# Attention with a recurrence beside it: where sinks and the fourth far tile are turned within a round

## The chip, the core and the metric

The kernel runs on one core of a Trainium2 chip. The metric is device time in microseconds for one execution. Before the change the median of three runs is 2368.65 us (2368.1 to 2369.14).

## The reference

A block of attention and a gated recurrence, for 4 sequences of 1024 tokens and 1024 channels in fp32. Attention has 16 query heads over 4 key heads of 64 channels, a sliding window of 512 keys, and 4 sink keys that every query sees. Cut to what matters:

```python
xn = _layernorm(x)
# attention
mask = (j <= i) & (j >= i - 511) | (j < 4)      # and causal for the first rows
att = softmax(where(mask, einsum('bkgqd,bkjd->bkgqj', q, k) / 8, -inf))
s = (att @ v) @ Wo.T
# recurrence: on the last token of each sequence, four steps
thought = layer_norm(xn)[:, -1, :] @ agg_w + agg_b
for _ in range(4):
    t = gelu(layer_norm(thought) @ d1_w + d1_b)
    thought = thought + t @ d2_w + d2_b
gate = sigmoid(xn @ gate_w + gate_b)
g = silu(layer_norm(xn + gate * (thought @ bc_w + bc_b)))
out = x + s * g
```

## The kernel before

The program has three stages. The first normalizes x and computes keys, values, queries and gates. The second, which the change touches, computes attention, and beside it the recurrence, whose weights are streamed from memory. The third multiplies by `Wo`, applies the gate and adds x.

**Rounds.** A tile is 128 queries. Attention takes query tiles in pairs (`PAIRED`): a *far* tile, the fifth to eighth of its sequence, whose window has left the start, and a *near* tile, the first to fourth. For a pair it takes 2 pairs of key heads and 2 halves of a group's heads, so 4 rounds for each of 16 pairs, 64 rounds in all. A `Step` is one tile in one round: two query heads for each of two key heads. A far step always has four turned key tiles (the first one holds the leading and the own keys laid over each other by a predicated copy) and four sink keys besides. A near step has 1, 2, 3 or 4 key tiles: the first pair of each sequence has 1, the fourth has 4.

**What a step does.** Line numbers are those of the profile.
- `scores` (L267): products of queries and keys into the PSUM tile `S` (four banks, one buffer). VectorE lays own keys over leading ones (L272), then adds the mask, scales and reduces (L289, with the extreme `nm`); ScalarE takes the exponential and sums it (L294). A far step does it in two halves, `scores((0,))` and `scores((1,))`, both into the one buffer; a near step at once.
- `normalized` (L301, L305): reciprocal of the sums, and the rows `pr` times it, on VectorE.
- `turned(k)` (L312): four 128x128 transposes into one PSUM tile, then a copy to `pT` by ScalarE (L316). For tile 0 of a far step VectorE also makes `lead` from the copy (L322).
- `turned_sinks` (L334): the last 32 columns of four `pr` tiles are multiplied by an identity, each into its own 32 rows of one PSUM tile; ScalarE copies it to `sT` (L339).
- `values(k)` (L344): value products of key tile k into `yp`. `values_apart`: the products with the sinks (L361) and with `lead`.
- `stored` (L374): copy of `yp` by VectorE; each second one is followed by a DMA from GpSimd (L379).

**PSUM.** Turned tiles, turned sinks and the recurrence's own turned or summed results share tag "T" of pool `ps_t`, with two buffers; `S` has four banks, `yp` and the recurrence's sums (`ps_f`) one each. [...]`pT` has four buffers in SBUF, `lead` and `sT` one.

**The recurrence.** `ffn()` is a generator: each unit is either a block of streamed weights (four products of 128x512, each into 32 rows, L685, with the DMA of its block on SyncE's queue, L683), or a turning of summed rows (four transposes, L739) or a mean or variance product (L759). There are 173 units. `filler(slot)` issues what is due; a round has three slots, and units are spread over the first 60 rounds, so nearly every slot has one. The last four rounds have none.

**What sets the order.** Within the attention loop TensorE's order is the order of the program text (`manual_schedule` for that engine). The other engines' orders are set by the scheduler from its own estimates of when inputs are ready. A round interleaves the current far and near step with the scores of the next round's steps, from L897 to L929. The array works in a mode, given in the profile as rows*columns: transposes 128*128, scores 64*128, value products 128*64, sinks' turning and the streamed blocks of the recurrence 128*32.

Of the kernel before, what the change touches and what calls it, by code (L numbers as in the profile page):

```python
# [43 lines left out]
def recurrent_block_kernel(  # L44
# [92 lines left out]
    sink_values, leads = {}, {}  # L137

    def load_kv(b):

        pool = pools["odd" if b % 2 else "first"]
        kT = pool.tile([P, N_KV // 2, TT, P + SINK], F32, tag="kT", name=f"kT{b}")
        v = pool.tile([P, TT, KVD], F32, tag="v", name=f"v{b}")
        for h in range(TT // BLK):
            n, at = b * (TT // BLK) + h, slice(h * BLK, (h + 1) * BLK)
            for m in range(N_KV // 2):
                nc.sync.dma_start(
                    kT[:, m, at, SINK:], k_dram[n][:, m, :].rearrange("p (t k) -> p t k", k=P)
                )
            nc.sync.dma_start(v[:, at, :], v_dram[n])  # L150
        far = WINDOW // P
        nc.gpsimd.tensor_copy(
            kT[:, :, far:, :SINK],
            kT[:, :, 0:1, SINK : 2 * SINK].to_broadcast([P, N_KV // 2, TT - far, SINK]),
        )

        sinks = pools["first"].tile([P, PAIR, KVD], F32, tag="sinks", name=f"sinks{b}", bufs=2)
        nc.gpsimd.memset(sinks, 0.0)
        for g in range(2):
            for r in range(PAIR):  # L160
                end = (2 * g + r + 1) * QUAD
                nc.gpsimd.dma_start(
                    sinks[end - SINK : end, r, :].rearrange("p (m g c) -> p m g c", m=2, g=2)[
                        :, :, g, :
                    ],
                    v_dram[b * (TT // BLK)][:SINK, 0, :].rearrange(
                        "p (m g c) -> p m g c", m=2, g=2
                    )[:, :, g, :],
                )
        kTs[b], vs[b], sink_values[b] = kT, v, sinks  # L170

    def load_q(i):
        qTs[i] = pools["first"].tile([P, N_HEAD // 2, P], F32, tag="qT", name=f"qT{i}", bufs=4)
        n, j = divmod(i, BLK)
        nc.sync.dma_start(qTs[i], q_dram[n][:, :, j * P : (j + 1) * P])
# [44 lines left out]
    class Step:  # L220
# [132 lines left out]
            last = not self.far and k + 1 == len(self.keys)  # L353
            self.added(self.pT.pop(k), vs[self.b][:, self.keys[k], :], k == 0, last)

        def values_apart(self):

            for r in range(PAIR):
                for g in range(2):
                    cols = slice((2 * self.m + g) * HS, (2 * self.m + g + 1) * HS)  # L360
                    nc.tensor.matmul(  # L361
                        self.y[g * HS : (g + 1) * HS, r * P : (r + 1) * P],
                        sink_values[self.b][:, r, cols], self.sT,
                        start=False, stop=False, skip_group_check=True,
                    )
            self.added(self.lead, leads[self.i], False, True)

        def stored(self):
# [23 lines left out]
    def steps_of(tiles, m, rp):  # L392
        return [Step(i, m, rp) for i in tiles]
# [5 lines left out]
    with ExitStack() as a:  # L399
# [193 lines left out]
        for n in range(NBLK):  # L593
# [11 lines left out]
            for kind, w7, part in (  # L605
                (queries, wq7, 0), (queries, wq7, 1), (gates, wg7, 0), (gates, wg7, 1)
            ):
                if n == NBLK - 1 and kind is gates and part == 0:
# [8 lines left out]
                    far, near = steps_of(*order[0])  # L617
# [26 lines left out]
    with ExitStack() as a:  # L644
# [188 lines left out]
        def load_y(n, row):  # L833

            t = ws.tile([P, 2, KH, BT // 2], F32, tag="stream", name=f"y2_{n}_{row}")
            ys.setdefault(n, {})[row] = t
            for j in range(BLK // 2):
                nc.sync.dma_start(
                    t[:, :, :, j * P : (j + 1) * P],
                    y_dram[n * BLK + row * (BLK // 2) + j].rearrange(  # L840
                        "p (h c q) -> p h c q", h=2, c=KH
                    ),
                )
# [3 lines left out]
        def filler(slot):  # L847
            nonlocal ffn_done
            due = FFN_UNITS * (p * SLOTS + slot + 1) // (ffn_steps * SLOTS)
            while ffn_done < min(due, FFN_UNITS + 1):  # L850
                next(ffn_gen, None)
                ffn_done += 1

        with tc.manual_schedule(engines={mybir.EngineType.PE}):
            for p in range(len(order)):
                pair, within = divmod(p, per_pair)
                if within == 0:
                    b, t = divmod(pair, TT // 2)  # L860
                    i = PAIRED[pair][0]
                    own = i % TT
                    leads[i] = px.tile([P, KVD], F32, tag="leads", name=f"leads{i}", bufs=2)
                    nc.vector.tensor_tensor(
                        leads[i], vs[b][:, own - WINDOW // P, :], vs[b][:, own, :], ALU.subtract
                    )
                    if pair + 1 < len(PAIRED):
                        for i in PAIRED[pair + 1]:
                            load_q(i)
                    if t == 1 and b + 1 < B:  # L870
                        load_kv(b + 1)


                if 0 <= p - 2 * DT < 2 * DT:
                    c, g = divmod(p - 2 * DT, 2)
                    m, r = divmod(c, GROUP)
                    h = (2 * m + g) * GROUP + r
                    tc.keep_in_program_order(
                        nc.sync.dma_start(
                            wo_sb[g * HS : (g + 1) * HS, c, :],  # L880
                            wo[h // 4, h % 2 * HS : (h % 2 + 1) * HS,
                               h // 2 % 2 * D : (h // 2 % 2 + 1) * D],
                        )
                    )
                if p > 4 * DT:
                    for dst, minuend, subtrahend in islice(wo_parts, 1):
                        tc.keep_in_program_order(
                            nc.vector.tensor_tensor(dst, minuend, subtrahend, ALU.subtract)
                        )
                if p == ffn_steps:  # L890
                    for _ in ffn_gen:
                        pass
                    for row in range(2):
                        load_y(0, row)
                more = p + 1 < len(order)
                n_near = len(near.keys)
                far.turned(0)  # L897
                far.turned_sinks()
                if more:
                    far_next, near_next = steps_of(*order[p + 1])  # L900
                    far_next.scores((0,))
                for k in (1, 2):
                    far.turned(k)
                filler(0)
                for k in range(3):
                    far.values(k)
                far.turned(3)
                if more:
                    far_next.normalized((0,))
                    far_next.scores((1,))  # L910
                for k in range(min(2, n_near)):
                    near.turned(k)
                filler(1)
                far.values(3)
                far.values_apart()
                far.stored()
                for k in range(2, n_near):
                    near.turned(k)
                if more:
                    far_next.normalized((1,))  # L920
                    near_next.scores(both)
                for k in range(n_near):
                    near.values(k)
                if more:
                    near_next.normalized(both)
                near.stored()
                filler(2)
                if more:
                    far, near = far_next, near_next  # L929
# [276 lines left out]
```

## Time and profile before

| what | value |
|---|---|
| profiled execution, its own time | 2368.6 us |
| its span, first to last instruction | 2366.9 us |
| granted TensorE clock | 1.000 |
| attention stage (first to last transposition of `pr`) | 1039.7 to 1972.2 us |
| transposes t, TensorE | 1664, 245.0 us busy |
| copies pT, ScalarE | 416, 585 ns each |
| masks and reductions, VectorE (L289) | 512, 590 ns each |
| exponentials, ScalarE | 512, 639 ns each |
| normalizing, VectorE (L305) | 512, 437 ns each |
| `lead`, VectorE | 64, 686 ns each |
| y copy, VectorE | 128, 420 ns each |
| sinks' turning, TensorE | 512 records, 64 copies of 261 ns |

The span is what the trace covers; the profiled execution's own time is 1.7 us longer. Matmuls of TensorE are pipelined: their lengths overlap, and what a group takes is read from its first start to the next group's first start. An fp32 product that isn't a transposition shows as two records. The number in brackets behind a row is idle time of the engine just before it, with what ended it.

### The profile page before, as it was taken

To read this page: it belongs to the slowest core of one execution; us is meant where nothing else is said; L and a number is where in the kernel's file an instruction comes from. 1 tells how busy PE (TensorE), PEld (TensorE's weight loads), DVE (VectorE), ACT (ScalarE), POOL (GpSimd) and SP (SyncE) were. 2 spreads that over 40 slices of the span, in tenths; PEclk is the share of its full clock that TensorE was granted. 3 is DMA by queue.
4 is the path that set the end of the run, shared out by engine and by line. 5 is a ranking of instruction groups with operands and counts; after the bars stand their busy time and mean duration, and the time that the engine had idled before them with its cause. 6 is when DMAs were issued, how large, how long until landed. Compare 5 with 4: busy or idle time off the path is not lost.

```text
span 2366.9 us, 31507 instructions
## 1 busy us (share of the span) xinstructions
PE 2324.0 (98%) x11966; PEld 1353.1 (57%) x11966; DVE 1226.0 (52%) x2973; ACT 865.4 (37%) x1960; POOL 322.9 (14%) x480
## 2 busy tenths in 40 slices
PE   7999999999999999999999999999999999999999
PEld 5757585757576666745555555555555554444444
DVE  7222222131212211147767767777777776777776
ACT  1110101010111111056666666666656664333332
POOL 2121313121212221320001000100000000111110
PEclk9999999999999999999999999999999999999999
DMA  8243111111111111346667777667466634667563
GB/s 338 96 172 125 62 59 62 45 72 49 60 52 66 49 54 40 112 157 210 201 199 233 249 218 227 204 213 231 155 215 219 215 89 165 176 192 201 153 170 89
DMA packets 190129, 348.79 MB, mean 147 GB/s; under 512 B 10789, under 2 KB 84597, under 8 KB 188441
## 3 DMA queue, kind: packets, MB, share of 16 engines
q1 hardware_dynamic: 161448, 252.74, 33.1%
q0 software_dynamic: 23200, 74.63, 10.3%
q10 hardware_dynamic: 5328, 19.40, 2.2%
q8 instruction: 94, 1.54, 0.3%
q14 instruction: 59, 0.48, 0.1%
HBM read 271.20 MB, written 92.31 MB: 154 GB/s over the span
## 4 chain that ended last, share of the span: by engine, by line
PE 80%; issue 14%; DVE 2%; ACT 2%; DMA 1%; POOL 1%; SPq 0%; ACTq 0%; POOLq 0%; DVEq 0%
PE u_q L538 16%; PE u L1044 15%; PE u_g L559 14%; PE S L267 6%; PE yp L344 6%; PE t L312 6%; PE kp L472 5%; PE vp L461 4%; PE d_ps L685 4%; PE xtp L450 1%; PE yp L361 1%; PE st L334 1%; DMA out_beta_sb<-in_out_beta_dram 1%; ACT pr L294 1%; POOL y_dram L379 0%
## 5 line engine op out<-in xcount | busy, mean ns | idle before, releaser
L294 ACT ACTIVATE pr<-pr,nm 128x516 f32<-128x516 f32 (+4 forms) x512 | 325.3, 639 | 137.8 <-DVE nm L289 137.1
L316 ACT COPY pT<-t 128x512 f32<-128x512 f32 x416 | 230.5, 585 | 218.1 <-PE t L312 216.8
L289 DVE CUSTOM_DVE_ANT_0 pr<-S,near_mask 128x516 f32<-128x516 f32 (+4 forms) x512 | 278.2, 590 | 36.7 <-PE S L267 32.1
L267 PE MATMUL S<-kT,qT 64*128 64x512 f32 (+4 forms) x1536 | 259.7, 456 | 2.7 <-DVE nm L289 2.7
L312 PE MATMUL t<-ident,pr 128*128 128x128 f32 x1664 | 245.0, 282 | 5.6 <-ACT pT L316 3.8
L312 PEld LDWEIGHTS t<-ident,pr 128*128 128x128 f32 x1664 | 177.5, 141 | 99.1 <-issue 68.1
L344 PE MATMUL yp<-pT,v 128*64 128x256 f32 x1664 | 222.4, 391 | 2.1 <-ACT pT L316 1.8
L305 DVE TENSOR_SCALAR pr<-pr,ri 128x516 f32<-128x516 f32 (+4 forms) x512 | 199.2, 437 | 5.9
L267 PEld LDWEIGHTS S<-kT,qT 64*128 64x128 f32 x1536 | 129.6, 186 | 118.6 <-issue 100.3
L344 PEld LDWEIGHTS yp<-pT,v 128*64 128x64 f32 x1664 | 101.8, 136 | 148.1 <-issue 68.3
L538 PE MATMUL u_q<-xT,wq_sb 128*128 128x256 f32 x768 | 172.2, 379 | 0.0
L559 PE MATMUL u_g<-wg_sb,xT 128*128 128x512 f32 x384 | 171.5, 592 | 0.0
L1044 PE MATMUL u<-wo_sb,y 128*128 128x512 f32 x384 | 170.1, 592 | 1.1 <-DVE y L374 1.1
L538 PEld LDWEIGHTS u_q<-xT,wq_sb 128*128 128x128 f32 x768 | 144.8, 190 | 22.5 <-issue 3.8
L451 ACT COPY xT<-xtp 128x512 f32<-128x512 f32 x64 | 37.5, 588 | 285.2 <-PE xtp L450 285.2
L379 POOL DMA_DIRECT2D y_dram<-y x64 | 35.6, 556 | 751.2 <-DVE y L374 735.8
L1044 PEld LDWEIGHTS u<-wo_sb,y 128*128 128x128 f32 x384 | 72.9, 190 | 92.9 <-issue 91.4
L559 PEld LDWEIGHTS u_g<-wg_sb,xT 128*128 128x128 f32 x384 | 71.8, 190 | 81.4 <-issue 80.6
L566 POOL TENSOR_TENSOR t_g<-t_g,gate_b_sb 128x512 f32<-128x512 f32 x64 | 87.1, 1361 | 195.8 <-DVE t_g L513 144.0
L538 PE MATMUL u_q<-s,wq_t 128*128 128x256 f32 x512 | 113.1, 379 | 0.0
L559 PE MATMUL u_g<-wg_t,s 128*128 128x512 f32 x256 | 112.7, 593 | 0.0
L461 PE MATMUL vp<-wv_sb,xT 128*128 128x256 f32 x512 | 112.6, 380 | 0.0
(198 smaller groups left out, 2971.3 us busy)
## 6 DMA issues: line engine op xcount, KB each, us to landing
d_w<-in_d_w_dram SPq DMA_DIRECT2D x128, 1024.0 KB, 5.9
xn<-in_x_dram ACTq DMA_DIRECT2D x34, 512.0 KB, 5.0
x<-in_x_dram SPq DMA_DIRECT2D x32, 512.0 KB, 3.9
q_dram<-t_q POOLq DMA_DIRECT2D x64, 256.0 KB, 2.6
g_dram<-t_g POOLq DMA_DIRECT2D x64, 256.0 KB, 2.3
qT<-q_dram SPq DMA_DIRECT2D x32, 512.0 KB, 4.8
y_dram<-y POOLq DMA_DIRECT2D x64, 256.0 KB, 4.3
y<-y_dram SPq DMA_DIRECT2D x32, 512.0 KB, 4.6
```

Of the source, the lines that this page charges most:

```text
L267: nc.tensor.matmul(S[:, dst, g, at_s], qTs[self.i][half[g], at + r, :], k, start=True, stop=True,)
L289: nc.vector.tensor_tensor_reduce(out=low, in0=S[:, src, g, :cols], in1=self.mask, scale=-1.0 / HS**0.5, scalar=-NEG, op0=ALU.add, op1=ALU.min,
L294: nc.scalar.activation(low, low, AF.Exp, bias=nm, scale=-1.0, accum_out=self.sums[:, r, g : g + 1],)
L305: nc.vector.tensor_scalar(at, at, rinv[:, r, g : g + 1], None, ALU.mult)
L312: nc.tensor.transpose(ps[:, g, r, :], self.pr[g][:, r, k * P : (k + 1) * P], ident)
L316: nc.scalar.copy(self.pT[k], ps.rearrange("p g r q -> p g (r q)"))
L344: nc.tensor.matmul(self.y[g * HS : (g + 1) * HS, :], v[:, cols], pT[:, g, :], start=first, stop=last,)
L461: nc.tensor.matmul(ps[:, h, :], xT[:, c, (j + h) * P : (j + h + 1) * P], wv_sb[:, c, :], start=(c == 0), stop=(c == DT - 1),)
L472: nc.tensor.matmul(ps, wk_sb[:, c, m * P : (m + 1) * P], xT[:, c, :], start=(c == 0), stop=(c == DT - 1),)
L538: nc.tensor.matmul(bank[:, h * (BT // 2) : (h + 1) * (BT // 2)], w7[i][:, c, at], left[n][i][:, c, :], start=(first and h == 0 and c == 0) ...
L559: nc.tensor.matmul(bank, left[n][i][:, c, j * P : (j + 1) * P], w7[i][:, c, :], start=(first and c == 0), stop=(c == KH - 1), skip_group_c ...
L1044: nc.tensor.matmul(bank, left[n][i][:, c, j * P : (j + 1) * P], wo7[i][:, c, :], start=(first and c == 0), stop=(c == KH - 1), skip_group_ ...
```

## The change

Within a round the order of TensorE's program changes in three places.
- `turned_sinks` of the far step is issued ahead of `turned(0)`, so directly behind the recurrence unit of the round before's last slot, `filler(2)`.
- `turned(3)` of the far step moves from ahead of the next round's `normalized((0,))` and `scores((1,))` to behind them, where it is followed by the near step's `turned(0)`.
- The near step's second tile, which was turned beside its first, is turned with the later ones, behind the far step's stored result. With one near tile nothing is left there.

`values_apart` is split into `sink_values` and `lead_values`, which are called one after the other in the same place.

```diff
-        def values_apart(self):
+        def sink_values(self):
             for r in range(PAIR):
                 for g in range(2):
...
+        def lead_values(self):
+
             self.added(self.lead, leads[self.i], False, True)
...
                 more = p + 1 < len(order)
                 n_near = len(near.keys)
+                far.turned_sinks()
                 far.turned(0)
-                far.turned_sinks()
                 if more:
                     far_next, near_next = steps_of(*order[p + 1])
                     far_next.scores((0,))
                 for k in (1, 2):
                     far.turned(k)
                 filler(0)
                 for k in range(3):
                     far.values(k)
-                far.turned(3)
                 if more:
                     far_next.normalized((0,))
                     far_next.scores((1,))
-                for k in range(min(2, n_near)):
-                    near.turned(k)
+                far.turned(3)
+                near.turned(0)
                 filler(1)
                 far.values(3)
-                far.values_apart()
+                far.sink_values()
+                far.lead_values()
                 far.stored()
-                for k in range(2, n_near):
+                for k in range(1, n_near):
                     near.turned(k)
```

With four near tiles a round's groups on TensorE are, before: tile 0 | sinks | scores 0 | tiles 1, 2 | unit | values 0 to 2 | tile 3 | scores 1 | near 0, 1 | unit | values 3, sinks, lead | near 2, 3 | near scores | near values | unit. After: sinks | tile 0 | scores 0 | tiles 1, 2 | unit | values 0 to 2 | scores 1 | tile 3, near 0 | unit | values 3, sinks, lead | near 1, 2, 3 | near scores | near values | unit.

## What to expect, worked out ahead of the result

> **What bounds the kernel now.** Read first the page's head and its busy times, then the sums by stretch of the attention stage, then one round on TensorE in order of time.
>
> ```profile
> span 2366.9 us, 31507 instructions
> ...
> PE 2324.0 (98%) x11966; PEld 1353.1 (57%) x11966; DVE 1226.0 (52%) x2973; ACT 865.4 (37%) x1960; POOL 322.9 (14%) x480
> ```
>
> ```profile
> 1330.00:1700.00 370.00, 363.92 (x2921) 197.62 (x2920) 274.38 (x881) 230.65 (x595) 18.76 (x32) 1.00 0.67 213
> ```
>
> In this stretch of attention TensorE is busy 363.92 of 370 us, VectorE 274.38, ScalarE 230.65, at full clock. So TensorE sets the pace, and a change there counts for what it alters in TensorE's own sequence and for new waits of it. One round, three near tiles, no recurrence unit ahead of it:
>
> ```profile
> 1415.53 0.66 PE L312 MATMUL t<-ident,pr 128*128 128x128 f32 x4
> 1416.12 0.43 PE L334 MATMUL st<-ident,pr 128*32 128x128 f32 x8
> 1416.47 1.35 PE L267 MATMUL S<-kT,qT 64*128 64x512 f32 x8
> 1417.83 1.09 PE L312 MATMUL t<-ident,pr 128*128 128x128 f32 x8
> 1418.86 1.07 PE L685 MATMUL d_ps<-d_w,hid_cols 128*32 128x512 f32 x8
> 1419.85 1.52 PE L344 MATMUL yp<-pT,v 128*64 128x256 f32 x12
> 1421.30 0.66 PE L312 MATMUL t<-ident,pr 128*128 128x128 f32 x4
> 1421.88 1.35 PE L267 MATMUL S<-kT,qT 64*128 64x512 f32 x8
> 1423.17 1.09 PE L312 MATMUL t<-ident,pr 128*128 128x128 f32 x8
> 1424.19 1.07 PE L685 MATMUL d_ps<-d_w,hid_cols 128*32 128x512 f32 x8
> 1425.19 0.65 PE L344 MATMUL yp<-pT,v 128*64 128x256 f32 x4
> 1425.67 0.61 PE L361 MATMUL yp<-sT,sinks 128*64 128x128 f32 x8
> 1426.11 0.60 PE L344 MATMUL yp<-lead,leads 128*64 128x256 f32 x4
> 1426.64 0.66 PE L312 MATMUL t<-ident,pr 128*128 128x128 f32 x4
> 1427.22 1.56 PE L267 MATMUL S<-kT,qT 64*128 64x384 f32 x8
> ```
>
> Columns: start, length, engine, line, operands, the array's mode (rows*columns), records. Read start to next start. Four transposes take 0.59 (1421.30 to 1421.88), eight take 1.02 (1423.17 to 1424.19): four more cost 0.435, so a group pays 0.15 beside its work. The value products say the same: twelve 1.45, and eight and sixteen in other rounds 1.02 and 1.88. Three products of one mode in a row (1425.19, 1425.67, 1426.11: 0.48 + 0.44 + 0.53 = 1.45) cost no more than twelve in one group. So it is the **change of mode** that costs 0.145.
>
> [...]The rows show 0.145 per change of mode, and nothing between products of one mode; I take the rows.
>
> **Part 1, groups.** No matmul, copy or DMA is added or removed; the order changes. Counted over 64 rounds in TensorE's two instruction orders:
> - The fourth far tile (t, 1421.30) goes behind the scores and joins the near tile's first: one group less in 47 rounds. With two near tiles (16 rounds) the second near tile now stands alone behind the value products, so nothing is saved there; the last round has no scores between.
> - Sinks (128*32) directly behind a recurrence unit of weight streaming (128*32): 43 rounds, one group less.
> - In 14 rounds the unit ahead is a turning or a mean or variance product (128*128), which before joined the far tile's first: one group more. The last round saves one.
> 47 + 43 - 14 + 1 = 77 groups x 0.145 = **-11.2 us**. No row has sinks behind a stream; the bounds are half (the start, 0.06, and the end, 0.09, of a group are each part of 0.145) and full. I take full, since the three products in a row above join fully.
>
> **Part 2, the third tile in a row waits.** Turned tiles have two PSUM buffers; a third must wait until ScalarE has copied the first. With four near tiles the groups were two and two; now n0 stands with the far tile, and n1, n2, n3 follow each other. The last round of before has just that sequence:
>
> ```profile
> 1967.91 1.09 PE L312 MATMUL t<-ident,pr 128*128 128x128 f32 x8
> 1969.30 0.66 PE L312 MATMUL t<-ident,pr 128*128 128x128 f32 x4 [0.30 <-ACT pT L316]
> 1969.88 0.65 PE L344 MATMUL yp<-pT,v 128*64 128x256 f32 x4
> ```
>
> 1.97 from 1967.91 to 1969.88, against 12 x 0.109 + 0.15 = 1.46 without the wait: 0.51. Behind it on TensorE stand the near scores and near products, so nothing covers it. 16 rounds have four near tiles; 12 of them, the last four apart: **+6.1**.
>
> **Part 3, the last four rounds.** They have no recurrence units, and VectorE holds the second scores:
>
> ```profile
> 1939.46 1.35 PE L267 MATMUL S<-kT,qT 64*128 64x512 f32 x8 [0.59 <-DVE nm L289]
> ```
>
> The far tile stood before this wait and was hidden in it; now it follows. From these scores to the near ones before: 1.29 + 1.02 + 1.45 + 1.02 = 4.78. After: 1.29 + 1.39 (value product 3 waits for the copy of the tile just turned) + 1.45 + 1.97 = 6.10. From near scores to the next second scores VectorE's chain sets the time, unchanged. 1.32 x 3 + 0.44 (their three groups, counted in part 1) + 0.2 in the last round = **+4.6**.
>
> **Part 4, smaller waits.**
> - Where a turned result ahead is still read by VectorE, its buffer is what the second tile of the round needs:
>
> ```profile
> 1105.93 0.60 PE L312 MATMUL t<-ident,pr 128*128 128x128 f32 x4
> 1106.81 0.42 PE L334 MATMUL st<-ident,pr 128*32 128x128 f32 x8 [0.28 <-DVE hid_cols L747]
> ```
>
> Before, 0.36 of sinks followed the release, now 0.585 of a far tile: 0.225, of which 0.145 is counted above; 13 rounds: +1.0.
> - One near tile (16 rounds): where the unit in slot 1 is a turning or a mean, it is now third in a row: 4 x 0.52. Where slot 1 is empty (three rounds, one with three near tiles), value product 3 waits for its copy: 3 x 0.37. Together +3.2.
> - The second scores stand 0.585 earlier behind the first, and need VectorE's two reductions of the first. Taking the start of these scores less the end of the reductions in each round, most have 0.9 to 2.0 us; seven, with three or four near tiles, have 0.42 to 0.62. Less 0.585, 0.06 for the semaphore and up to 0.145 (a joined group), seven rounds stall 0.03 to 0.33: +1.5.
> - VectorE's order in the changed kernel puts the far y copy behind a normalization (0.49) in most rounds with one near tile, and both behind exponentials that ScalarE now starts about 0.6 later, after two tile copies. With S1's end as zero: copies to 1.8, exponentials to 3.3, reciprocal, one normalization, y ready at 4.4; the near products want it at 1.02 + 1.0 + 1.45 + 0.65 = 4.1. Six rounds x 0.35 = +2.1. Bounds: 0 if ScalarE is early, 16 x 0.4 = 6.
> The SP queue keeps its order but for one k load; GpSimd swaps a copy with two sink loads, far ahead of use: nothing.
>
> **The sum.** -11.2 + 6.1 + 4.6 + 1.0 + 3.2 + 1.5 + 2.1 = +7.3. The profiled execution took 2368.6 (span 2366.9 and 1.7 around it), the median of the runs is 2368.65, so the same base: **2375.9 us**, 0.3% slower. Its own range: without the last two waits and with half of part 3, 2370; with half of the sinks' joining lost (+3.1) and the y waits at their bound, 2382.
>
> **Rivals.**
> - *The groups decide (faster).* If the waits of parts 3 and 4 are hidden, by ScalarE and VectorE moving along with TensorE, -11.2 + 6.1 gives 2363.5; if n3's wait is hidden too, 2357.4. For it: VectorE has 26% idle, and ScalarE 38%. Against: n3's copy cannot start before n1 is turned, and the row in part 2 shows the price with ScalarE idle before it. It decides if n3's gap is under 0.2. Chance 0.18.
> - *A draw.* Groups as counted, parts 2 and the firm waits of part 4 (4.2) as counted, part 3 half: -11.2 + 6.1 + 4.2 + 2.3 = +1.4, 2370. For it: the reductions and the y copy are the least certain terms. Chance 0.22.
> - *Joining does not happen (slower still).* The sinks wait for their buffer or for normalized rows, so a stream and sinks drain between as before: 43 x 0.145 = 6.2 is lost, 2382. Against: the buffer's copy ended a unit earlier. Chance 0.10, counted as slower.
> The forecast has 0.50. About 0.2% (4.7 us) can be told from no change. Slower 0.60, same 0.22, faster 0.18. The range that holds 8 in 10: 2362 to 2382.
>
> **What would show it.** Right: sinks starting about 0.86 after a stream's start instead of 1.0; far tile and near tile as one group of eight, 1.02; in rounds with four near tiles eight transposes, then a gap near 0.3 ended by the pT copy, then four; in the last rounds 6.1 from second to near scores. Wrong: no gap before n3, or a busy TensorE in attention that falls by 11 us with idle time unchanged. The forecast fails if a round with four near tiles is not longer than before.

## The result and the profile after

The changed kernel takes 2375.07 us (median of 10 runs, 2373.07 to 2377.49), the kernel before, run on the same chip, 2368.39 us (median of 10, 2368.10 to 2369.59). The ratio is 1.0026, with an interval of 1.0017 to 1.0035: **slower by 0.26%**. The forecast was 2375.9. The profiled execution took 2375.14 us, of which 2373.4 are its span, so it is 6.5 us longer than the span of before (2366.9). Runs of every kernel fall into two clusters some 1.5 us apart, which the last section traces to one stretch of 3.4 us at half clock; compared cluster with cluster, the changed kernel is 5.0 us slower.

The head of the page of the changed kernel, and its sum for the same stretch of attention (columns: stretch, its length, then busy time and records of TensorE, its weight loads, VectorE, ScalarE and GpSimd, then granted clock, DMA share, GB/s):

```profile
span 2373.4 us, 31542 instructions
...
PE 2318.4 (98%) x11966; PEld 1358.8 (57%) x11966; DVE 1225.1 (52%) x2973; ACT 864.9 (36%) x1960; POOL 321.9 (14%) x480
```

```profile
1330.00:1700.00 370.00, 361.30 (x2920) 199.95 (x2918) 274.34 (x880) 230.94 (x597) 18.23 (x32) 1.00 0.67 214
```

TensorE is busy 5.6 us less than before (2324.0 to 2318.4), with as many records, and yet the span is 6.5 us longer: the work became cheaper, and idle time grew by 12.1 us (span less busy: 42.9 before, 55.0 now). In the stretch its idle time went from 6.08 us (370 less 363.92) to 8.70. The sums by line say which operations the waits stand ahead of (the last column is idle time just before the group, and what ended most of it). First before, then the changed kernel:

```profile
L267 PE MATMUL S<-kT,qT 64*128 64x512 f32 (+4 forms) x1536 | 259.7, 456 | 2.7 <-DVE nm L289 2.7
L312 PE MATMUL t<-ident,pr 128*128 128x128 f32 x1664 | 245.0, 282 | 5.6 <-ACT pT L316 3.8 <-DVE t_g L525 0.9 <-ACT sT L339 0.6
L344 PE MATMUL yp<-pT,v 128*64 128x256 f32 x1664 | 222.4, 391 | 2.1 <-ACT pT L316 1.8 <-DVE y L374 0.3
L334 PE MATMUL st<-ident,pr 128*32 128x128 f32 x512 | 27.3, 284 | 7.2 <-DVE hid_cols L747 4.0 <-ACT pT L316 1.5 <-DVE var L764 0.8
```

```profile
L267 PE MATMUL S<-kT,qT 64*128 64x512 f32 (+4 forms) x1536 | 260.5, 457 | 7.3 <-DVE nm L289 7.0
L312 PE MATMUL t<-ident,pr 128*128 128x128 f32 x1664 | 238.3, 281 | 13.9 <-ACT pT L316 4.7 <-DVE hid_cols L750 3.5 <-ACT sT L339 2.1
L344 PE MATMUL yp<-pT,v 128*64 128x256 f32 x1664 | 223.2, 392 | 5.9 <-ACT pT L316 4.1 <-DVE y L377 1.8
L334 PE MATMUL st<-ident,pr 128*32 128x128 f32 x512 | 26.2, 277 | 0.9 <-DVE t_g L528 0.9
```

Scores wait 4.6 us more, above all for VectorE's reductions; value products wait 3.8 us more, for copies of turned tiles and of `yp`. The 8.3 us more ahead of transposes are for the most part no new waits: 6.3 us of waiting left the sinks (7.2 to 0.9), since the far tile is now what stands behind a turned result that is still being read.

One round with four near tiles, on TensorE in order of time; first some rows of before, then the changed kernel:

```profile
1249.83 0.66 PE L312 MATMUL t<-ident,pr 128*128 128x128 f32 x4
1250.42 1.35 PE L267 MATMUL S<-kT,qT 64*128 64x512 f32 x8
1251.70 1.09 PE L312 MATMUL t<-ident,pr 128*128 128x128 f32 x8
1252.72 1.07 PE L685 MATMUL d_ps<-d_w,hid_cols 128*32 128x512 f32 x8
...
1255.17 1.09 PE L312 MATMUL t<-ident,pr 128*128 128x128 f32 x8
1256.19 1.99 PE L267 MATMUL S<-kT,qT 64*128 64x512 f32 x8
```

```profile
1244.59 1.06 PE L688 MATMUL d_ps<-d_w,hid_cols 128*32 128x512 f32 x8
1245.48 0.40 PE L334 MATMUL st<-ident,pr 128*32 128x128 f32 x8
1245.81 0.66 PE L312 MATMUL t<-ident,pr 128*128 128x128 f32 x4
...
1251.14 1.35 PE L267 MATMUL S<-kT,qT 64*128 64x512 f32 x8
1252.43 1.09 PE L312 MATMUL t<-ident,pr 128*128 128x128 f32 x8
1253.45 1.07 PE L688 MATMUL d_ps<-d_w,hid_cols 128*32 128x512 f32 x8
...
1255.90 1.09 PE L312 MATMUL t<-ident,pr 128*128 128x128 f32 x8
1257.29 0.66 PE L312 MATMUL t<-ident,pr 128*128 128x128 f32 x4 [0.29 <-ACT pT L316]
1257.87 1.99 PE L267 MATMUL S<-kT,qT 64*128 64x512 f32 x8
```

(Lines behind L365 have moved by three.) Sinks start 0.89 behind the stream's start, where a stream and its successor were 1.00 apart: two groups of one mode do join. The fourth far tile and the first near one are one group of eight, 1.02 (1252.43 to 1253.45). And the three near tiles behind the value products take 1.97 (1255.90 to 1257.87), with the gap of 0.29 ended by a copy, where two took 1.02 before.

In the last rounds the far tile follows the second scores, and the value product behind it waits for its copy. The near scores of the same round before (its second scores, at 1939.46, are shown in the forecast), then the changed kernel:

```profile
1944.25 1.99 PE L267 MATMUL S<-kT,qT 64*128 64x512 f32 x8
```

```profile
1942.73 1.35 PE L267 MATMUL S<-kT,qT 64*128 64x512 f32 x8 [1.49 <-DVE nm L289]
1944.02 1.09 PE L312 MATMUL t<-ident,pr 128*128 128x128 f32 x8
1945.40 0.65 PE L344 MATMUL yp<-pT,v 128*64 128x256 f32 x4 [0.29 <-ACT pT L316]
...
1948.83 1.99 PE L267 MATMUL S<-kT,qT 64*128 64x512 f32 x8
```

From second to near scores are 6.10 us (4.78 before). TensorE now comes to the second scores with less work behind it, but waits there for VectorE, 1.49 instead of 0.59, so moving the tile gave nothing ahead of them.

Round by round (scores to the same scores of the next round), after less before, the sums over rounds 0 to 62 are:

| rounds | number | after less before, us | a usual round |
|---|---|---|---|
| one near tile | 16 | +2.31, of it +1.59 in round 0 | -0.29 without a wait, 0.0 to +0.4 with one |
| two near tiles | 16 | -1.25 | -0.14 |
| three near tiles | 16 | -3.17 | -0.29 |
| four near tiles, with recurrence | 12 | +4.12 | +0.22 |
| four near tiles, the last ones | 3 | +4.20 | +1.40 |

That is +6.2 in all; the remaining 0.3 of 6.5 lies ahead of the first and behind the last of these scores. The gain of joining is there, 0.14 or 0.15 a time, and more than it is lost again where four near tiles stand, above all in the last rounds. Round 0 is no part of the change; its 1.5 us are taken up in the last section.

### The profile page after: what moved, and what is told of

Same layout as the page of the kernel before. It is cut to its first block, busy times and chain, and to the rows that moved or that the text cites. A ratio compares the mean times of both kernels' runs of the same rounds, so it can differ in the third digit from the quotient of the medians.

```text
span 2373.4 us, 31542 instructions
## 1 busy us (share of the span) xinstructions
PE 2318.4 (98%) x11966; PEld 1358.8 (57%) x11966; DVE 1225.1 (52%) x2973; ACT 864.9 (36%) x1960; POOL 321.9 (14%) x480
## 4 chain that ended last, share of the span: by engine, by line
PE 87%; DVE 4%; ACT 3%; issue 3%; DMA 2%; POOL 1%; SPq 0%; ACTq 0%; POOLq 0%; DVEq 0%
PE u_q L541 16%; PE u L1048 15%; PE u_g L562 14%; PE S L267 9%; PE yp L344 8%; PE t L312 7%; PE d_ps L688 5%; PE kp L475 5%; PE vp L464 4%; ACT pT L316 1%; DVE pr L289 1%; ACT pr L294 1%; PE xtp L453 1%; PE yp L361 1%; DVE pr L305 1%
## 5 line engine op out<-in xcount | busy, mean ns | idle before, releaser
L312 PE MATMUL t<-ident,pr 128*128 128x128 f32 x1664 | 238.3, 281 | 13.9 <-ACT pT L316 4.7
L1048 PE MATMUL u<-wo_t,s 128*128 128x512 f32 x256 | 112.5, 592 | 0.0
```

The lines of the kernel that those rows point to most:

```text
L312: nc.tensor.transpose(ps[:, g, r, :], self.pr[g][:, r, k * P : (k + 1) * P], ident)
L1048: nc.tensor.matmul(bank, left[n][i][:, c, j * P : (j + 1) * P], wo7[i][:, c, :], start=(first and c == 0), stop=(c == KH - 1), skip_group_ ...
```

## The experiments

Each is compared with the kernel before, run beside it; its median was 2369.60 for the first four, 2368.49 for the next four and 2368.67 for the last two. Edits are shown by what they amount to, against the kernel that each names. "Groups" are stretches of TensorE's program in one mode, counted over the attention loop.

### The sinks alone

To the kernel before, only this:

```diff
-                far.turned(0)
-                far.turned_sinks()
+                far.turned_sinks()
+                far.turned(0)
```

> The sinks alone turned ahead of the round's first far tile; the tiles as before. Joining theory (a change of mode costs 0.145 us, nothing else moves): 30 groups less than before, -4.35, and +1.0 where a turned result ahead holds its buffer: 2365.1 us, with a stream followed by sinks 0.14 shorter than before and no other step changed. Rival, late chain (the far tile that is now second starts lead and its copies later, and that is what made the change slower): slower than before, 2370 or more. Rival, no joining (sinks drain the stream anyway): 2369 to 2371.

Measured: 2364.43 against 2369.60, ratio 0.9979 (0.9970 to 0.9987), -5.2 us; cluster with cluster -5.4. The change of mode is real and the sinks do join: TensorE's groups of one mode fall from 869 to 839. Both rivals fall: the one under which joining doesn't happen, and the one under which the later copies make it slower. But the gain is some 2 us larger than the sum said, and one piece of the surplus is in the rounds behind a turned result of the recurrence. Before and this kernel, the same round; the bracket is idle time and what ended it:

```profile
1385.20 0.43 PE L334 MATMUL st<-ident,pr 128*32 128x128 f32 x8 [0.81 <-DVE hid_cols L747]
1385.56 1.35 PE L267 MATMUL S<-kT,qT 64*128 64x512 f32 x8
1387.65 1.09 PE L312 MATMUL t<-ident,pr 128*128 128x128 f32 x8 [0.74 <-ACT pT L316]
```

```profile
1384.68 0.63 PE L312 MATMUL t<-ident,pr 128*128 128x128 f32 x4 [0.90 <-DVE hid_cols L747]
1385.24 1.35 PE L267 MATMUL S<-kT,qT 64*128 64x512 f32 x8
1386.81 1.14 PE L312 MATMUL t<-ident,pr 128*128 128x128 f32 x8 [0.22 <-ACT sT L339]
```

The recurrence's transposes began at 1383.29 and 1382.77. The scores come 2.27 and 2.47 behind them: the release costs the +0.2 that was foreseen. But then the second key tile waits for the small copy of the sinks and no longer for the large one of a tile: 0.22 instead of 0.74. So the loss was more than paid back, which the forecast had not seen.

### The tiles alone

To the kernel before, only the moves of `turned(3)` and of the near step's second tile, sinks left behind tile 0.

```diff
-                far.turned(3)
                 if more:
                     far_next.normalized((0,))
                     far_next.scores((1,))
-                for k in range(min(2, n_near)):
-                    near.turned(k)
+                far.turned(3)
+                near.turned(0)
...
-                for k in range(2, n_near):
+                for k in range(1, n_near):
                     near.turned(k)
```

> The fourth far tile and the near tiles moved as in the change; sinks as before. Joining theory: 47 groups less, -6.8, and waits of third tiles +6.1, last four rounds +4.6, smaller waits +6.4: 2378.7 us, with four near tiles eight transposes, a gap near 0.3 ended by the copy, and four. Rival, late chain of the sinks: the tiles are not to blame, 2368 or less.

Measured: 2379.03 against 2369.60, ratio 1.0038 (1.0024 to 1.0052), +9.4 us; cluster with cluster some +9 where +10.3 was expected. The loss of the change is all here; the sinks are its gain. Groups fall by 47 to 822, as counted, and the kernel is slower nevertheless. The two parts don't quite add up: -5.4 and +9 make less than the +5.0 of the whole change. What they do to each other was not isolated.

### Rounds with four near tiles in their old order

The changed kernel, but rounds with four near tiles (16, the last four among them) turn their tiles as before:

```diff
+                moved = n_near < 4
+                if not moved:
+                    far.turned(3)
                 if more:
                     far_next.normalized((0,))
                     far_next.scores((1,))
-                far.turned(3)
-                near.turned(0)
+                if moved:
+                    far.turned(3)
+                beside = 1 if moved else min(2, n_near)
+                for k in range(beside):
+                    near.turned(k)
```

> The changed kernel, but rounds with four near tiles keep the old order of tiles. Third-tile theory: relative to the changed kernel -6.1 and -4.6 and -1.2 of stalls of the second scores, +1.7 for 12 groups: 2364.9 us, faster than before. Rival, spread-out small waits (every round a little later): a quarter of the rounds gives back a quarter of the loss, 2373.

Measured: 2364.54 against 2369.60, ratio 0.9977 (0.9969 to 0.9986), -5.1 us. Undoing the tiles in a quarter of the rounds turns the loss into a gain, although 15 of the joined groups are given up with it; the rival of waits spread over all rounds falls. Parts 2 and 3 of the forecast together decide the sign. The time is that of the sinks alone (-5.2): in the other 48 rounds the moved tiles bring nothing in sum.

### The last near tile behind the near scores

In the changed kernel, with four near tiles, the last one is turned behind the near scores, in a group of its own. No third turned tile stands in a row then: if the copy is what costs, 0.51 goes and one group comes back.

```diff
-                for k in range(1, n_near):
+                apart = n_near == 4
+                for k in range(1, n_near - apart):
                     near.turned(k)
                 if more:
                     far_next.normalized((1,))
                     near_next.scores(both)
+                if apart:
+                    near.turned(3)
```

> The changed kernel, but with four near tiles the last near tile is turned behind the near scores, a group of its own (15 groups more), so that it never is third in a row. Two-buffer theory: a group of 0.145 in place of a wait of 0.51 in 12 rounds (-4.4), and 0.95 less from the second to the near scores in three of the last four (-2.8): 2367.9 us. Rival, the wait comes from ScalarE being late with n1 because of the exponentials, or from the number of transposes behind lead: no gain, and 15 groups more, 2377.

Measured: 2370.05 against 2369.60, ratio 1.0002 (0.9994 to 1.0010). A usual round gains 0.36 to 0.37 on the changed kernel, which is 0.51 less the 0.145 of one group more: the wait for the copy is the price, at its predicted size. The kernel as a whole gains 5 us on the changed kernel where 7.2 were expected. One reason is that the near scores can also be short. In three rounds the next pair has one near tile, so its scores take 0.64 instead of 1.9, and no longer cover the copy of the tile behind them. One of these rounds:

```profile
1743.06 0.71 PE L267 MATMUL S<-kT,qT 64*128 64x128 f32 x8
1743.70 0.66 PE L312 MATMUL t<-ident,pr 128*128 128x128 f32 x4
1744.29 1.51 PE L344 MATMUL yp<-pT,v 128*64 128x256 f32 x12
1746.32 0.65 PE L344 MATMUL yp<-pT,v 128*64 128x256 f32 x4 [0.52 <-ACT pT L316]
```

Three value products are done, the fourth waits 0.52 for its tile's copy. The last rounds gained only 0.57 each, where 0.95 was expected; the reason stays open. A tile moved to where a long group covers its copy needs the group to be long in every round: scores of 1.9 us covered it here, scores of 0.64 did not.

### Sinks only where a stream is ahead of them

The kernel before, with sinks first in all rounds but the 14 in which a turning, a mean or a variance product stands ahead.

```diff
-                far.turned(0)
-                far.turned_sinks()
+                if p not in {1, 3, 5, 17, 19, 24, 31, 38, 41, 45, 50, 52, 55, 58}:
+                    far.turned_sinks()
+                    far.turned(0)
+                else:
+                    far.turned(0)
+                    far.turned_sinks()
```

> Sinks ahead of the first far tile only in rounds that don't follow a turned or summed result; tiles as before. Joining theory: 44 groups less than before at 0.145: -6.4 us against before, and none of the rounds longer than before. Rival, the gain of turning the sinks alone came from elsewhere (the rounds behind turned results, where later waits got shorter): less than -3.4.

Measured: 2362.12 against 2368.49, ratio 0.9974 (0.9964 to 0.9983), -6.4 us; cluster with cluster -6.5. Groups fall by 44 to 825, and 44 x 0.145 = 6.4. This is the cleanest measurement of the price of a change of mode: in the trace no round is longer than before, and nearly all that joined a group are shorter by 0.13 to 0.15. The rival, that the gain came from the rounds behind turned results, falls.

### Only the parts that gain

The kernel before, in which each round takes an edit only where its own trace had gained: sinks first in 50 rounds (24 among them, 0 not), the tiles' move in rounds with three near tiles (not 8 and 43, which had a stall) and in rounds 3, 19 and 35.

```diff
+                if p not in {0, 1, 3, 5, 17, 19, 31, 38, 41, 45, 50, 52, 55, 58}:
+                    far.turned_sinks()
+                    far.turned(0)
...
+                moved = n_near == 3 and p not in (8, 43) or p in (3, 19, 35)
```

> Sinks first only where a stream is ahead (and in one round behind a turned result), the tiles' move only with three near tiles and in three rounds with one, where the slots hold streams and the scores have room: 60 groups less than before at 0.145, no third tile in a row added: -8.7 us against before, the fastest so far. Rival, small waits move elsewhere (the second scores, the y copy): -5 to -6.

Measured: 2361.07 (2359.90 to 2361.38) against 2368.49, ratio 0.9966 (0.9953 to 0.9978), **-7.4 us**, the fastest of all and faster than both kernels. The median lies between the forecast of -8.7 and its rival's -5 to -6; cluster with cluster it is -8.4 or more, so with the forecast. TensorE has 809 groups there, 17 more than in the changed kernel, and the kernel is some 13 us faster than that one, cluster with cluster. Fewer groups are no aim by themselves.

### The last four rounds in their old order

The changed kernel with this condition in place of `n_near < 4` above, so that rounds 60 to 63 turn their tiles as before:

```diff
+                moved = p < ffn_steps
```

> The changed kernel, with the old order of tiles in the last four rounds alone. Theory of part 3: -4.6 against the changed kernel, so +2.1 against before, with 4.8 instead of 6.1 from second to near scores there. Rival, these rounds hang on VectorE and TensorE's order is hidden in them: no gain, +6.7 against before.

Measured: 2369.99 against 2368.49, ratio 1.0004 (0.9996 to 1.0012). Cluster with cluster that is 4.8 to 5.0 less than the changed kernel, by a change in four rounds of 64. The far tile turned ahead of the second scores is hidden again in the wait for VectorE:

```profile
1939.58 1.35 PE L267 MATMUL S<-kT,qT 64*128 64x512 f32 x8 [0.81 <-DVE nm L289]
...
1944.36 1.99 PE L267 MATMUL S<-kT,qT 64*128 64x512 f32 x8
```

Second to near scores are 4.78 again. The rival, that these rounds hang on VectorE alone with TensorE's order hidden in them, falls.

### Rounds with one near tile in their old order

The changed kernel with this condition, so that rounds with one near tile turn their tiles as before:

```diff
+                moved = n_near > 1
```

> The changed kernel, with the old order of tiles in rounds with one near tile. Theory of part 4: there the joined group saves 16 x 0.145 = 2.3 and waits (third tile, empty slot, y copy, second scores) cost more; by the trace of the changed kernel the move costs 2.5 net in these rounds: -2.5 against the changed kernel, +4.2 against before. Rival, the joined group decides: +2.3, so +9 against before.

Measured: 2373.07 against 2368.49, ratio 1.0016 (1.0010 to 1.0023), cluster with cluster about 1.8 us less than the changed kernel, where 2.5 was expected. In these 16 rounds the waits outweigh the groups. It doesn't separate the waits for the y copy from those of a third tile in a row: no run moves the y copy alone, and that term stands on rows of the trace.

### The changed kernel once more, and round 0

The changed kernel unchanged, and the changed kernel with the old order in round 0 alone, to see whether the new order there brings on the slower cluster.

> The changed kernel once more, beside before on one chip. Theory of the clock: runs of both fall into two groups about 1.4 us apart, by whether TensorE's clock is halved for 3.4 us in the first attention round; within the same group the changed kernel is 5 us longer than before (about 2373.4 and 2374.9 against 2368.4 and 2369.8), and the rest of the 6.7 between the medians is that more of its runs were in the upper group. Rival, the two groups are chance of the chip and of equal share in both: the medians differ by 5.

> The changed kernel, with the old order in the first attention round alone (one group of TensorE more). If the changed order of that round brings on the clock's halving, the share of upper runs falls to that of before, and the median is 1 to 1.5 below the changed kernel's on this chip. Rival, the wait for the copies in that round is in both kernels, and so the halving: no difference beyond 0.3.

Measured: 2374.99 against 2368.67, ratio 1.0023 (1.0015 to 1.0031), and 2374.59, ratio 1.0024 (1.0016 to 1.0033). The two don't differ by more than they scatter, and each had 9 of 13 runs in the upper cluster, so the order of round 0 is not shown to do it. Within each cluster the changed kernel, run again, is 5.0 and 5.1 us above before, as expected.

## Why the forecast held

By its own steps:

- **TensorE sets the pace.** Right: new waits on it show in the time, at full length (0.51 us for the third tile in a row, as forecast, and 1.40 a round in the last rounds, for 1.32) but for those that shorten a later wait (see the sum).
- **Part 1, groups (-11.2).** Right in count (869 to 792 groups), in price and in full joining, which was a choice between half and full. Sinks: 44 groups gave 6.4 us alone. Tiles: a round with three near tiles is 0.15 shorter by them, one with two is unchanged.
- **Part 2, third tile in a row (+6.1).** Right: 1.97 where 1.97 was forecast, 0.51 a round before the group saved, in 12 rounds; a usual round of the experiment with the last near tile behind the near scores isolates it.
- **Part 3, last rounds (+4.6).** Right: 6.10 for 6.10. The three rounds between cost +4.2 together, 1.40 each for 1.32, and the last round next to nothing. With the groups counted in part 1 put back (0.44, and about 0.2 in the last round) that is 4.8 for 4.6. Undoing the tiles there alone gave 4.8 to 5.0.
- **Part 4.** The release of turned results: +0.20 to +0.23 where 0.225 was forecast, in the eight of 13 rounds where it can be read apart. The third turned result with one near tile: 0.51 in rounds 2, 16, 32 and 34, and 0.35 in two rounds with an empty slot, 2.7 in all for 3.2. Second scores: eight rounds stall 0.10 to 0.45, some 2.2 for 1.5. The y copy: six rounds, 1, 18, 33 and 48 to 50, stall 0.23 to 0.28, so 1.6 for 2.1; in one of them, in the timeline of the changed kernel,

```profile
1760.87 0.71 PE L267 MATMUL S<-kT,qT 64*128 64x128 f32 x8
1761.84 0.65 PE L344 MATMUL yp<-pT,v 128*64 128x256 f32 x4 [0.26 <-DVE y L377]
```

  the near product waits for `yp` to be copied out, at 0.97 instead of 0.69 behind the scores.
- **The sum (+7.3).** Too high by some two us: with clocks alike the difference is about 5. A term that it lacked has the other sign: where a turned result had stood ahead, waits later in the next round shrink (round 24 by 0.47; rounds 31, 38, 45 and 52 by 0.21 to 0.24; 1.4 in all). Round 24's was shown in the first experiment. In rounds 31 and 45 the streamed block behind it waits for its column operands in any case, 0.72 and 0.74 before, 0.49 and 0.50 now; in rounds 38 and 52 the second key tile waited 0.29 and 0.28 for the copy of the sinks and waits no longer. So what is lost ahead is regained there; that is read from the trace and not isolated. Summed with the measured terms: -11.2 + 6.1 + 4.8 + 1.0 + 2.7 + 2.2 + 1.6 - 1.4 = +5.8. The rounds of the trace, without the 1.6 of round 0, give +4.6, so about 1 us of these small terms is not accounted for; the 1.0 for the release, taken from eight rounds, is the least certain. The top of the forecast's range, by its own terms, is 2382.9 and not 2382.
- **The base.** The rest of the measured 6.7 is not the change's own mechanism but the clock in round 0: of the runs of before beside the result 2 of 10 were in the upper cluster, of the changed kernel's 8 of 10. That the forecast's median came within 0.8 us is partly luck: this and the lacking term cancel.
- **The rivals.** That groups decide fell with the last near tile's gap of 0.29, above the 0.2 that it needed. The draw fell as its uncertain terms, the reductions and the y copy, came at about their forecast size (2.2 and 1.6). That joining doesn't happen fell with the sinks alone.

## What to carry to other kernels

Price a change of array mode from the trace (group against group, start to start; 0.145 us here), but keep a reordering only in rounds where the moved tile's copy is still covered by what follows: with two PSUM buffers a third turned tile in a row cost its wait in full, 0.51 us here. Where an engine waits for another, work that stands ahead of the wait can be free and cost its time behind it (in the last rounds here 4.78 us from second to near scores became 6.10); look for such rounds separately, as at the end of a loop, where filler work has run out. Cluster with cluster, the edits chosen for each round by its own trace gave -8.4 us, where the same edits applied to all gave +5.0.

## What the runs showed of the hardware besides

TensorE's clock halves for one stretch of round 0, 3.4 us long, in some executions. Eight of the twelve profiled ones show it; before's profile does not, but its runs have the same two clusters. The sums for 1046 to 1052 us, of the kernel before and of the changed one (the clock is the third number from the end):

```profile
1046.00:1052.00 6.00, 5.40 (x46) 3.27 (x48) 3.11 (x9) 3.35 (x8) 0.00 (x0) 1.00 1.04 397
```

```profile
1046.00:1052.00 6.00, 5.45 (x28) 2.87 (x30) 2.48 (x6) 1.80 (x5) 0.00 (x0) 0.72 1.06 397
```

From 1047.00 to 1049.50 the changed kernel's clock is 0.50:

```profile
1047.00:1049.50 2.50, 2.50 (x10) 1.09 (x8) 0.00 (x0) 0.00 (x0) 0.00 (x0) 0.50 1.05 408
```

So a mean of 0.72 over 6 us is a clock of 0.5 for 6 x 0.28 / 0.5 = 3.4 us. It follows an idle wait; the changed kernel's rows:

```profile
1046.32 1.88 PE L344 MATMUL yp<-pT,v 128*64 128x256 f32 x8 [2.07 <-ACT pT L316]
1048.12 2.20 PE L267 MATMUL S<-kT,qT 64*128 64x512 f32 x8
```

Scores that take 1.35 elsewhere take 2.20. What sets the halving off was not shown. One pair of profiles has the same order and the same wait in round 0, with the halving in one and not in the other: the kernel with only its last four rounds in the old order has round 0 in the changed order, waits the same 2.07 us there, and kept its full clock (1.00):

```profile
1046.00:1052.00 6.00, 5.48 (x48) 3.38 (x48) 3.09 (x9) 3.20 (x8) 0.00 (x0) 1.00 1.05 394
```

Its round 0 (scores to scores) took 14.50 us, the changed kernel's 16.08. So the halving costs about 1.5 us, which is the distance between the two clusters; single runs at 0.998 and 0.997, some 2 to 4 us longer, fit two or three such stretches, though none was profiled. In all, 44 of 103 runs of before and 17 of 23 of the changed kernel were in the upper cluster. The length of the wait alone doesn't decide: of the eight profiles with the halving six had waited 2.07 us and two 1.80, of the four without it (before among them, with 1.81) two and two. Whether the slightly longer wait raises the share was not settled: round 0 in its old order didn't lower it. For a kernel of this kind it means that differences of under 1.5 us are read within a cluster, or not at all.
